# Cross-attention: one four-bank PSUM tile becomes four tiles, and some work of the other engines moves

## The chip, the cores and the metric

The kernel runs on one core of a Trainium2 chip. A core has five engines that run side by side, each through its own queue in order: TensorE (PE in the profile; its weight loads are PEld), VectorE (DVE), ScalarE (ACT), GpSimd (POOL) and SyncE (SP, which here only issues DMAs). TensorE writes its results to PSUM; the kernel's four banks of sums lie there. The metric is the device time of one execution in microseconds (us), lower is better.

## The reference

For each of 64 sequences (256 rows of queries `x`, 512 wide; 256 rows of context `c`, 384 wide), in float32:

```python
text_p  = einsum('bld,dh->blh', x, W_text) + b_text      # 512 -> 512
audio_p = einsum('bsd,dh->bsh', c, W_audio) + b_audio    # 384 -> 512
Q = layer_norm(text_p, g1, beta1)
K = layer_norm(audio_p, g2, beta2)
V = audio_p
scores = einsum('blh,bsh->bls', Q, K) / sqrt(512)
alpha  = softmax(scores, axis=-1)
hyper  = einsum('blh,hk->blk', einsum('bls,bsh->blh', alpha, V), W_out) + b_out
return layer_norm(hyper + x, g_out, beta_out)
```

## The kernel before

The whole program is unrolled, with its order written by hand: the order of the calls in the source is the order in each engine's queue, and the framework adds the semaphore waits that the data need. One sequence is one round of the main loop (line 1027), and a round works on several sequences at once. In round `b` it computes keys (`k2`) and queries (`q2`) of sequence `b + 2`, the scores and the exponentials of `b` (`at`), the context (`alpha` times `c`) of `b - 1` (`last`), the output product of `b - 2` (`old.o`), and the closing layer norm and store of `b - 3` (`settled`).

The value product and `W_out` are folded at the start (`fold_multiply`): the context rows are multiplied by `W_audio W_out`. So there are three large products for a sequence.

- Keys and output rows go through the class `Thirds` (line 482): a product of 2 by 3 by 3 blocks with 15 block products in place of 18. Its sums are 172 wide, and there are eight of them: L0, L1, M0, M1, N0, N1, T, U. TensorE adds products to them in five steps, `one` (N), `two` (M), `three` (T), `four` (M, L, T), `five` (N, M, U). Between these, VectorE works on the sums in PSUM: `after_one` (copy N1, write T), `after_three` (copy T, write L), `after_four` (write U). `after_five`, `leave` and `leave_plus` take the results out. `seed` (line 508) writes the bias into M before `two`. Keys and output share the same sums, one after the other in the round.
- Queries go through the class `Fork` (line 569): a product of 2 by 2 by 2 blocks with 7 block products, with sums in two further banks (`fork`). `first`, `six`, `five`, `rest` are its steps on TensorE; `after_first` copies two of the sums on ScalarE. `square`, `scales` and `normalise` make the layer norm; the rows are scaled where they leave PSUM.

The eight sums of `Thirds` lie in one PSUM tile of four banks (line 65), at these places:

```python
third = p_all.tile([P, 4, H], F32, tag="third", name="ps_t")
L0, M0 = third[:, 0, :W3], third[:, 0, W3 : 2 * W3]
T, U = third[:, 1, :W3], third[:, 1, W3 : 2 * W3]
L1, M1 = third[:, 2, :W3], third[:, 2, W3 : 2 * W3]
N0, N1 = third[:, 3, :W3], third[:, 3, W3 : 2 * W3]
```

Normalised queries and keys are stored to DRAM (`qd`, `kd`) and fetched again in squares (`qq`, `kq`) that VectorE's transposing instruction turns (`turn`, lines 74 and 453) into `qT` and `kT`; ScalarE then applies gamma and beta to them (`affine`, line 469). The exponentials take the same way (`ed`, `eq`, `turn_e`, `eT`). Inputs come as rows (`x`, `c`) and as squares (`xq`, `cq`), the squares four rounds ahead. All of these DMAs are issued by SP, in this order in a round: `eq`, `x`, `c`, `cq`, `xq`, `qd`, `kd`, `qq`, `kq`, `ed`, `out`.

GpSimd makes the sums of blocks that the fast products need: `third_sides` (line 306) for keys (`csum`) and for the output (`zsum`), `sum_x` (line 290) for queries (`xsum`); it also makes the reciprocal square roots (`rstd_of`, line 362) and part of the rows.

Of the kernel before, what the change touches and what calls it, by code (L numbers as in the profile page):

```python
# [9 lines left out]
F32 = mybir.dt.float32  # L10
AF = mybir.ActivationFunctionType
ALU = mybir.AluOpType
# [3 lines left out]
P = 128  # L16
# [6 lines left out]
def kernel(  # L23
# [18 lines left out]
    nc = tc.nc  # L42
    ctx.enter_context(tc.manual_schedule())
    B, L, D = x.shape
    S, DA = c.shape[1:]
    H = w_text.shape[1]
    LT, ST = L // P, S // P
    DC, AC, HC = D // P, DA // P, H // P
    scale = 1.0 / math.sqrt(H)
    W3 = -(-H // 12) * 4  # L50
# [11 lines left out]
    p_all = ctx.enter_context(tc.tile_pool(name="p_all", bufs=1, space=PSUM))  # L62
    p_at = ctx.enter_context(tc.tile_pool(name="p_at", bufs=2, space=PSUM))

    third = p_all.tile([P, 4, H], F32, tag="third", name="ps_t")
    fork = p_all.tile([P, 2, H], F32, tag="fork", name="ps_f")

    def squares(dst, src):
# [163 lines left out]
    wao_sb = wao_pad[:, :, :D]  # L232
# [4 lines left out]
    def fold_multiply(a, lo=0, hi=HC):  # L237

        for k in range(lo, hi):
            nc.tensor.matmul(  # L240
                third[:, a, :],
                lhsT=waT[k][:, bass.ts(a, P)],
                rhs=wo_sb[:, k, :],
                start=(k == 0),
                stop=(k == HC - 1),
            )

    def fold_evict(a):
        nc.scalar.copy(wao_sb[:, a, :], third[:, a, :])

    def fold_bias(part):

        ps = third[:, 3, :]
        nc.tensor.matmul(ps, lhsT=ones, rhs=part, start=True, stop=True)
        nc.vector.tensor_copy(bao_sb, ps)

# [222 lines left out]
    def dve(o, i0, i1, op):  # L479
        nc.vector.tensor_tensor(o, i0, i1, op)  # L480

    class Thirds(Projection):

        L0, M0 = third[:, 0, :W3], third[:, 0, W3 : 2 * W3]
        T, U = third[:, 1, :W3], third[:, 1, W3 : 2 * W3]
        L1, M1 = third[:, 2, :W3], third[:, 2, W3 : 2 * W3]
        N0, N1 = third[:, 3, :W3], third[:, 3, W3 : 2 * W3]
        L, M, N = third[:, 0:3:2, :W3], third[:, 0:3:2, W3 : 2 * W3], third[:, 3, : 2 * W3].rearrange("p (n h) -> p n h", n=2)

        def __init__(self, name, b, sides, weights, bias, delta):  # L490
            self.name, self.b, self.nt, self.centred = name, b, 2, True
# [37 lines left out]
        def after_one(self):  # L529
            n1 = self.room("n1")  # L530
            nc.vector.tensor_copy(n1, self.N1)  # L531
            dve(self.T, self.N0, n1, ALU.subtract)
# [9 lines left out]
            dve(m, self.M1, self.delta, ALU.subtract)  # L542
            dve(self.U, self.M0, m, ALU.subtract)

        def after_five(self):
            u, n = self.room("u"), self.room("n", 2)
            nc.scalar.copy(u, self.U)
            nc.scalar.copy(n, self.N)  # L548
            dve(self.rows[:, 0, W3 : 2 * W3], self.T, u, ALU.add)
            dve(self.ends(1), self.M, n, ALU.add)  # L550
            d = self.room("d")
            nc.gpsimd.tensor_tensor(d, n[:, 0], n[:, 1], ALU.subtract)  # L552
            nc.gpsimd.tensor_tensor(self.rows[:, 1, W3 : 2 * W3], u, d, ALU.add)

        def ends(self, t):
            return self.padded[:, t].rearrange("p (j h) -> p j h", j=3)[:, 0:3:2]
# [12 lines left out]
    class Fork(Projection):  # L569
# [20 lines left out]
            self.product(1, self.R)  # L590
            self.product(7, self.q2)

        def after_first(self):
            nc.scalar.copy(self.q1, self.R)
            self.s7 = once.tile([P, H2], F32, tag="s7", name="s7")
            nc.scalar.copy(self.s7, self.q2)  # L596

# [34 lines left out]
    class Attention:  # L632
# [114 lines left out]
            self.y = self.o.rows  # L747

        def statistics(self, lo=0, n=LT):

            self.nm = small.tile([P, LT], F32, tag="nm", name="nm")
            self.ssq = small.tile([P, LT], F32, tag="ssq", name="ssq")
            self.summed = range(lo, lo + n)
            for t in self.summed:
                junk = work.tile([P, D], F32, tag="junk", name="junk")
                nc.scalar.activation(  # L756
                    junk, self.y[:, t, :], AF.Identity, scale=-1.0 / D, accum_out=self.nm[:, t : t + 1]
                )
            for t in self.summed:
                junk = work.tile([P, D], F32, tag="junk", name="junk")  # L760
                nc.scalar.activation(  # L761
                    junk,
                    self.y[:, t, :],
                    AF.Square,
                    bias=self.nm[:, t : t + 1],
                    accum_out=self.ssq[:, t : t + 1],
                )
            self.r = dict(zip(self.summed, rstd_of(self.ssq[:, lo : lo + n], n, total=True)))
# [137 lines left out]

    assert B > 4 and AC == 3
    q, k, xT, cT, xs, cs, att = {}, {}, {}, {}, {}, {}, {}
    bank = [third[:, n, :] for n in range(4)] + [fork[:, n, :] for n in range(2)]

    c_turn = RowTurn(c_0, AC, "cT")
    x_turn = RowTurn(x_0, DC, "xT")
# [77 lines left out]
    k[0].affine(g2_sb, be2_sb)  # L990
    q[1] = Fork(1, xs.pop(1), wt_blocks)
    q[1].first()
    q[1].after_first()
    part = bias_parts()
    fold_multiply(2, 0, 2)
    q[1].six()
# [22 lines left out]
    wao_room = const.tile([P, HC * H], F32, tag="wo", name="wao_thirds")  # L1019
    wao_t = wao_room[:, : 11 * W3].rearrange("p (n h) -> p n h", n=11)  # L1020

    def start_queries(b):
        q[b] = Fork(b, xs.pop(b), wt_blocks)
        q[b].first()
        q[b].after_first()

    for b in range(B - 2):
        at = att[b] = att.get(b) or Attention(b)
        settled, old, last = att.pop(b - 3, None), att.get(b - 2), att.get(b - 1)
        three = b + 3 < B  # L1030
        if last:
            last.fetch_e()
        if b > 1:
            load_x_rows(b - 1)
            load_c_rows(b - 1)
        if b + 4 < B:
            load_c(b + 4)
            load_x(b + 4)
        if b == 1:
            go_sb = row(g_out, "go")  # L1040
            beo_sb = row(beta_out, "beo")
        if b == 0:
            at.score(0, 8)
            Fork.seed()
        k2 = k[b + 2] = Thirds("k", b + 2, cs.pop(b + 2), wa_blocks, ba_pad, ba_delta)
        if b == 0:
            k2.seed()
        k2.one()
        k2.after_one()
        k2.two()  # L1050
        if b == 0:
            start_queries(2)
        q2 = q[b + 2]
        if old:
            old.context_two(0)
        k2.three()
        if old:
            old.context_two(1)
            old.copy_two()
        if three:  # L1060
            cT[b + 3] = turn_c(b + 3)
        if b:
            at.affine_keys()
        k2.after_three()
        if old:
            old.start_products()
        if three:
            cs[b + 3] = third_sides(cT.pop(b + 3), "csum")
        q2.six()
        q2.after_six()  # L1070
        k2.four()
        k2.after_four()
        q2.five()
        q2.after_five()
        if last:
            last.turn_e()
        if b:
            at.affine_queries()
        k2.five()
        if settled:  # L1080
            settled.statistics()
        k2.after_five()
        q2.rest()
        k2.leave()
        if old:
            old.o.seed()
        q2.square()
        q2.scales()
        q[b + 1].turn()
        if three:  # L1090
            xT[b + 3] = turn_x(b + 3)
        if b:
            at.score(0, 2)
        if old:
            old.o.one()
            old.o.after_one()
            old.o.two()
        if b:
            at.score(2, 3)
        if old:  # L1100
            old.o.three()
        k[b + 1].turn([0])
        k2.square()
        k2.scales()
        if old:
            old.o.after_three()
        k[b + 1].turn([1])
        if not three:
            att[b + 1] = Attention(b + 1)
            att[b + 1].affine_queries()  # L1110
        if b:
            at.score(3, 6)
        q2.normalise()
        q2.store()
        if old:
            old.o.four()
        if settled:
            settled.shift(0)
            settled.shift(1)
        if old:  # L1120
            old.o.after_four()
        if b:
            at.score(6, 8)
        if old:
            old.o.five()
        if three:
            Fork.seed()
        k2.normalise()
        k2.store()
        q2.fetch()  # L1130
        k2.fetch()
        if three:
            xs[b + 3] = sum_x(xT.pop(b + 3))
        if b < 2:
            wao_blocks = third_weights(wao_pad, wao_t, [b])
        at.maxima()
        at.exponentials()
        if not three:
            att[b + 1].affine_keys()
        if settled:  # L1140
            settled.settle(0)
        if old:
            old.o.after_five()
        if three:
            start_queries(b + 3)
        at.reciprocals()
        if old:
            old.o.leave_plus(x_rows[b - 2])
        if last:
            last.context_one()  # L1150
        at.divide_e()
        if three:
            k2.seed()
        at.store_e()
        if last:
            last.copy_one()
        if settled:
            settled.settle(1)
            settled.store()

    settled, old, last = att[B - 5], att[B - 4], att[B - 3]
    at = att[B - 2]
# [46 lines left out]
    q[B - 1].affine(g1_sb, be1_sb)  # L1209
    end = Attention(B - 1)  # L1210
    old.o.five()
    old.o.after_five()
    old.o.leave_plus(x_rows[B - 4])
    last.o.seed()
    at.context()
# [17 lines left out]
    end.reciprocals()  # L1233
    old.statistics()
    last.o.five()
    last.o.after_five()
    last.o.leave_plus(x_rows[B - 3])
    end.transpose_e(bank[5])
    end.copy_e()
# [65 lines left out]
```

## Time and profile before

| what | value |
| --- | --- |
| median of 2 runs | 1824.55 us (1824.04 to 1825.06) |
| the profiled execution | 1824.55 us, its span 1822.8 us |
| mean granted TensorE clock | 0.931 |
| ScalarE copies of `s7` (L596), first to last of 63 | 48.9 to 1719.5 us |
| the chain of work that ended last, by engine | PE 54%, ACT 26%, DVE 8%, DMA 6% |
| DMA, share of the 16 engines' time | 71.3%, mean 177 GB/s |

A line of the profile names the engine, the source line, the tile written and the tiles read, and how often. `ps_t` is the tile `third`, `ps_f` is `fork`, `ps_sc` the scores, `ps_z` the context. A number in brackets behind a line of the timeline is the time that the engine sat idle before it, and what released it. The clock is that which the chip granted to TensorE, 1.00 being full speed. A call of the matmul shows as two rows.

### The profile page before, as it was taken

The numbers are of one execution on the slowest core, as the hardware profiler recorded it, in microseconds if no ns is written. First come the engines' busy times: TensorE is split into PE (matmuls) and PEld (weight loads), VectorE is DVE, ScalarE is ACT, GpSimd is POOL, SyncE is SP. The second block draws the span as 40 slices with busy tenths as digits, with TensorE's granted clock in tenths as the row PEclk, the third lists the DMA queues.
The fourth block names the chain that finished last, engine by engine and source line by source line (L and its number), as shares of the span: only waits on it lengthen the run. The fifth ranks groups of instructions, "written<-read, shape, count | busy, mean of one in ns | idle before, by whom it ended". The sixth has DMA issues, their size and how long they took to land.

```text
span 1822.8 us, 25850 instructions
## 1 busy us (share of the span) xinstructions
PE 1572.8 (86%) x7419; PEld 1314.6 (72%) x7419; DVE 1077.5 (59%) x2248; ACT 1143.7 (63%) x2929; POOL 1139.2 (62%) x1946
## 2 busy tenths in 40 slices
PE   7798988988988988988988988988988988988965
PEld 3577777777777777777777777777777777777753
DVE  4355665665665666665665665665665665665545
ACT  3466666666666667666666666666666666666651
POOL 4766566566566566566566566566566566566534
PEclk9899999999999999999999999999999999999988
DMA  7586767777877877877777777767777877777641
GB/s 186 122 191 167 202 173 174 202 174 174 203 173 175 203 171 179 200 170 179 198 173 180 195 175 181 198 172 181 197 172 181 199 171 181 197 173 179 168 142 47
DMA packets 450453, 322.51 MB, mean 177 GB/s; under 512 B 154885, under 2 KB 382981, under 8 KB 450310
## 3 DMA queue, kind: packets, MB, share of 16 engines
q1 hardware_dynamic: 450214, 320.72, 71.3%
q8 instruction: 59, 0.97, 0.2%
q14 instruction: 84, 0.69, 0.1%
q10 hardware_dynamic: 96, 0.13, 0.0%
HBM read 203.83 MB, written 116.92 MB: 176 GB/s over the span
## 4 chain that ended last, share of the span: by engine, by line
PE 54%; ACT 26%; DVE 8%; DMA 6%; issue 3%; POOL 1%; SPq 1%; DVEq 0%; ACTq 0%; POOLq 0%
PE ps_t L499 28%; PE ps_f L585 11%; PE ps_sc L650 11%; ACT junk L620 4%; ACT qT L471 3%; ACT kT L471 3%; PE ps_z L716 3%; ACT e L681 3%; ACT ps_t L509 3%; DVE ps_t L480 2%; DMA c<-in_ctx_dram 2%; DVE n L531 2%; ACT junk L756 2%; DVE kr L480 2%; ACT junk L761 2%
## 5 line engine op out<-in xcount | busy, mean ns | idle before, releaser
L650 PE MATMUL ps_sc<-kT,qT 128*128 128x256 f32 x1024 | 309.4, 432 | 4.2 <-ACT zT L731 4.2
L552 POOL TENSOR_TENSOR d<-n 128x172 f32<-128x172 f32 x124 | 68.1, 549 | 298.1 <-ACT n L548 293.4
L499 PE MATMUL ps_t<-wao,zsum 128*128 128x172 f32 x496 | 141.7, 424 | 128.1 <-DVE ps_t L480 71.7
L650 PEld LDWEIGHTS ps_sc<-kT,qT 128*128 128x128 f32 x1024 | 228.1, 231 | 26.5 <-ACT zT L731 5.0
L311 POOL TENSOR_TENSOR zsum<-zT 128x256 f32<-128x256 f32 x124 | 73.3, 591 | 242.8 <-ACT zT L734 231.5
L499 PEld LDWEIGHTS ps_t<-wao,zsum 128*128 128x128 f32 x496 | 101.0, 251 | 166.4 <-DVE ps_t L480 87.9
L667 ACT ACTIVATE e<-ps_sc,nmx 128x256 f32<-128x256 f32 x128 | 59.4, 469 | 238.2 <-DVE nmx L660 238.2
L585 PE MATMUL ps_f<-wtsum,xsum 128*128 128x256 f32 x756 | 197.0, 384 | 1.0 <-ACT s L596 0.6
L716 PE MATMUL ps_z<-eT,c 128*128 128x256 f32 x768 | 197.1, 381 | 0.8 <-ACT eT L705 0.8
L499 PE MATMUL ps_t<-wao_thirds,zsum 128*128 128x172 f32 x744 | 184.9, 347 | 2.5 <-DVE ps_t L480 2.5
L499 PE MATMUL ps_t<-wa,csum 128*128 128x172 f32 x496 | 107.5, 340 | 79.6 <-DVE ps_t L480 54.4
L499 PE MATMUL ps_t<-wa_thirds,csum 128*128 128x172 f32 x744 | 173.1, 328 | 0.0
L499 PEld LDWEIGHTS ps_t<-wao_thirds,zsum 128*128 128x128 f32 x744 | 142.1, 213 | 39.1 <-DVE ps_t L480 24.5
L499 PEld LDWEIGHTS ps_t<-wa,csum 128*128 128x128 f32 x496 | 74.6, 193 | 121.0 <-DVE ps_t L480 70.8
L536 DVE COPY t<-ps_t 128x172 f32<-128x172 f32 x124 | 41.8, 337 | 202.4 <-PE ps_t L499 202.4
L585 PEld LDWEIGHTS ps_f<-wtsum,xsum 128*128 128x128 f32 x756 | 143.1, 193 | 19.2 <-ACT s L596 0.9
L499 PEld LDWEIGHTS ps_t<-wa_thirds,csum 128*128 128x128 f32 x744 | 121.6, 191 | 42.7 <-DVE ps_t L480 39.5
L716 PEld LDWEIGHTS ps_z<-eT,c 128*128 128x128 f32 x768 | 141.5, 192 | 14.4 <-ACT eT L705 1.0
L734 ACT COPY zT<-ps_z 128x256 f32<-128x256 f32 x64 | 23.8, 372 | 199.5 <-PE ps_z L716 199.5
L370 POOL TENSOR_TENSOR rstd<-ve,nhalf 128x2 f32<-128x2 f32 (+1 forms) x192 | 136.1, 709 | 16.0
L585 PE MATMUL ps_f<-wt,xT 128*128 128x256 f32 x504 | 132.5, 386 | 10.2 <-ACT ps_f L581 10.2
L480 DVE TENSOR_TENSOR kr<-ps_t,u 128x172 f32<-128x172 f32 x62 | 20.9, 337 | 190.9 <-ACT n L548 114.4
(196 smaller groups left out, 4056.7 us busy)
## 6 DMA issues: line engine op xcount, KB each, us to landing
kd<-kr SPq DMA_DIRECT2D x64, 512.0 KB, 3.2
kq<-kd SPq DMA_DIRECT2D x256, 128.0 KB, 3.9
qd<-qr SPq DMA_DIRECT2D x64, 512.0 KB, 2.8
qq<-qd SPq DMA_DIRECT2D x256, 128.0 KB, 3.5
xq<-in_x_dram SPq DMA_DIRECT2D x252, 128.0 KB, 5.3
x<-in_x_dram SPq DMA_DIRECT2D x63, 512.0 KB, 4.2
out_dram<-yr SPq DMA_DIRECT2D x62, 512.0 KB, 3.1
cq<-in_ctx_dram SPq DMA_DIRECT2D x252, 96.0 KB, 5.4
```

Of the source, the lines that this page charges most:

```text
L311: less = lambda o, i0, i1: nc.gpsimd.tensor_tensor(o, i0, i1, ALU.subtract)
L370: nc.gpsimd.tensor_tensor(r, ve, nhalf[:, :n], ALU.pow)
L471: nc.scalar.activation(self.T[:, k, :], self.T[:, k, :], AF.Identity, bias=bet[:, k : k + 1], scale=gam[:, k : k + 1],)
L480: nc.vector.tensor_tensor(o, i0, i1, op)
L499: nc.tensor.matmul(place, lhsT=self.sides[n], rhs=self.weights[n], start=(n == 14), stop=True, skip_group_check=True,)
L509: nc.scalar.copy(self.M, self.bias.rearrange("p (j h) -> p j h", j=3)[:, 0:3:2])
L552: nc.gpsimd.tensor_tensor(d, n[:, 0], n[:, 1], ALU.subtract)
L585: nc.tensor.matmul(place, lhsT=side, rhs=w, start=False, stop=True, skip_group_check=True)
L620: nc.scalar.activation(junk, fork[:, t, :], AF.Square, scale=1.0 / math.sqrt(H), accum_out=self.var[:, t : t + 1],)
L650: nc.tensor.matmul(self.sc[:, t, :], lhsT=self.qT[:, k, bass.ts(t, P)], rhs=self.kT[:, k, :], start=(k == 0), stop=(k == HC - 1),)
L667: nc.scalar.activation(self.e[:, t, :], self.sc[:, t, :], AF.Exp, bias=self.nmx[:, t : t + 1], accum_out=self.den[:, t : t + 1],)
L716: nc.tensor.matmul(ps, lhsT=c_rows[self.b][:, s, bass.ts(j, P)], rhs=self.eT[:, s, :], start=(s == 0), stop=(s == ST - 1),)
```

## The change

The four banks become four tiles of their own, named m, l, u and n. Each holds a pair side by side: M0 and M1, L0 and L1, T and U, N0 and N1. The copies of `u` and `n` in `after_five` take the engine as an argument: ScalarE for keys, VectorE for the output in the main loop. The GpSimd part of it becomes `middle`. `after_first` of the queries is cut into `after_one` and `after_seven`, and `statistics` of the closing layer norm into `sums` and `deviations`. In the loop, `sums` go to the head of the round and `deviations` behind the scaling of the keys; the queries of sequence `b + 1` are scaled by gamma and beta in round `b`, between the squares and `normalise` of `q2`; GpSimd's `csum` goes behind `middle` of the keys; the squares of the keys go ahead of those of the queries; both `settle` go to the end of the round. The number of matmuls and of DMAs stays.

```diff
-    third = p_all.tile([P, 4, H], F32, tag="third", name="ps_t")
+    third = [p_all.tile([P, H], F32, tag=f"t{n}", name=f"ps_{n}") for n in "mlun"]
...
-        L0, M0 = third[:, 0, :W3], third[:, 0, W3 : 2 * W3]
-        T, U = third[:, 1, :W3], third[:, 1, W3 : 2 * W3]
-        L1, M1 = third[:, 2, :W3], third[:, 2, W3 : 2 * W3]
-        N0, N1 = third[:, 3, :W3], third[:, 3, W3 : 2 * W3]
-        L, M, N = third[:, 0:3:2, :W3], third[:, 0:3:2, W3 : 2 * W3], third[:, 3, : 2 * W3].rearrange("p (n h) -> p n h", n=2)
+        M, L, TU, N = [t[:, : 2 * W3].rearrange("p (n h) -> p n h", n=2) for t in third]
+        M0, M1, L0, L1 = M[:, 0], M[:, 1], L[:, 0], L[:, 1]
+        T, U, N0, N1 = TU[:, 0], TU[:, 1], N[:, 0], N[:, 1]
...
-        def after_five(self):
-            u, n = self.room("u"), self.room("n", 2)
-            nc.scalar.copy(u, self.U)
-            nc.scalar.copy(n, self.N)
-            dve(self.rows[:, 0, W3 : 2 * W3], self.T, u, ALU.add)
-            dve(self.ends(1), self.M, n, ALU.add)
+        def after_five(self, copy):
+            self.u, self.n = self.room("u"), self.room("n", 2)
+            copy(self.u, self.U)
+            copy(self.n, self.N)
+            dve(self.rows[:, 0, W3 : 2 * W3], self.T, self.u, ALU.add)
+            dve(self.ends(1), self.M, self.n, ALU.add)
+
+        def middle(self):
             d = self.room("d")
-            nc.gpsimd.tensor_tensor(d, n[:, 0], n[:, 1], ALU.subtract)
-            nc.gpsimd.tensor_tensor(self.rows[:, 1, W3 : 2 * W3], u, d, ALU.add)
+            nc.gpsimd.tensor_tensor(d, self.n[:, 0], self.n[:, 1], ALU.subtract)
+            nc.gpsimd.tensor_tensor(self.rows[:, 1, W3 : 2 * W3], self.u, d, ALU.add)
...
     for b in range(B - 2):
...
+        if settled:
+            settled.sums()
         k2.one()
         k2.after_one()
         k2.two()
...
         if old:
             old.start_products()
-        if three:
-            cs[b + 3] = third_sides(cT.pop(b + 3), "csum")
         q2.six()
         q2.after_six()
+        if settled:
+            settled.deviations()
         k2.four()
...
             last.turn_e()
-        if b:
-            at.affine_queries()
         k2.five()
-        if settled:
-            settled.statistics()
-        k2.after_five()
-        q2.rest()
+        k2.after_five(nc.scalar.copy)
         k2.leave()
+        k2.middle()
+        if three:
+            cs[b + 3] = third_sides(cT.pop(b + 3), "csum")
         if old:
             old.o.seed()
+        q2.rest()
+        k2.square()
         q2.square()
         q2.scales()
+        k2.scales()
         q[b + 1].turn()
...
         k[b + 1].turn([0])
-        k2.square()
-        k2.scales()
         if old:
             old.o.after_three()
...
             at.score(3, 6)
+        q[b + 1].affine(g1_sb, be1_sb)
         q2.normalise()
         q2.store()
...
-        if settled:
-            settled.settle(0)
         if old:
-            old.o.after_five()
+            old.o.after_five(nc.vector.tensor_copy)
+            old.o.middle()
         if three:
-            start_queries(b + 3)
+            q3 = q[b + 3] = Fork(b + 3, xs.pop(b + 3), wt_blocks)
+            q3.first()
+            q3.after_one()
         at.reciprocals()
...
         at.divide_e()
         if three:
+            q3.after_seven()
             k2.seed()
         at.store_e()
         if last:
             last.copy_one()
         if settled:
+            settled.settle(0)
             settled.settle(1)
             settled.store()
```

## The prediction

> **What bounds the kernel now.** I read the page first: busy time by engine and the clock row.
>
> ```profile
> span 1822.8 us, 25850 instructions
> PE 1572.8 (86%) x7419; PEld 1314.6 (72%) x7419; DVE 1077.5 (59%) x2248; ACT 1143.7 (63%) x2929; POOL 1139.2 (62%) x1946
> PEclk9899999999999999999999999999999999999988
> ```
>
> No engine but PE is above 63%, and PE itself never gets its whole clock: its mean is 0.931 in every slice. So the bound is PE with something that takes time from it in every round of the main loop. The copies of `s7` (L596) stand 27.31 us apart from 135.08 to 1719.5 us: 58 equal rounds. The timeline of PE over one of them, 899.9 to 927.2 us, with its idle time in brackets, is:
>
> ```profile
> 901.90 0.85 PE L499 MATMUL ps_t<-wa,csum 128*128 128x172 f32 x4 [0.33 <-ACT ps_t L509]
> 903.63 0.85 PE L499 MATMUL ps_t<-wa,csum 128*128 128x172 f32 x4 [0.88 <-DVE ps_t L480]
> 913.08 1.03 PE L650 MATMUL ps_sc<-kT,qT 128*128 128x256 f32 x4
> 915.06 0.82 PE L499 MATMUL ps_t<-wao,zsum 128*128 128x172 f32 x4 [0.95 <-POOL ve L366]
> 916.93 1.52 PE L499 MATMUL ps_t<-wao,zsum 128*128 128x172 f32 x4 [1.05 <-DVE ps_t L480]
> ```
>
> These four gaps, 0.33 + 0.88 + 0.95 + 1.05 = 3.21 us, are all the idle time of the round, and each stands before `one` or `two` of a `Thirds`. `one` writes N (fourth bank); what releases it is ACT's `seed` (L509), which writes M (first and third bank). `two` writes M; what releases it is DVE's subtraction that writes T (second bank). The third gap names POOL, but that `ve` ended at 914.58; the `seed` of the output ended at 914.96, 0.1 us before the matmul. So PE waits for an access to another bank of the same tile. The list of PE's waits has it for the whole run:
>
> ```profile
> PE ps_t L499 <- DVE ps_t L480: 128.6, 127, 8.0
> PE ps_t L499 <- POOL ve L366: 54.1, 57, 1.0
> PE ps_t L499 <- ACT ps_t L509: 25.2, 62, 3.2
> ```
>
> Then stretches of 1 us (PE's busy time, then PEld, DVE, ACT, POOL, clock, DMA share, GB/s):
>
> ```profile
> 915.90:916.90 1.00, 0.00 (x0) 0.00 (x0) 0.97 (x4) 1.00 (x5) 0.77 (x2) 0.99 0.03 5
> 916.90:917.90 1.00, 0.97 (x3) 0.97 (x4) 0.59 (x1) 0.73 (x3) 0.92 (x3) 0.50 0.00 0
> 918.90:919.90 1.00, 1.00 (x4) 0.91 (x4) 0.00 (x0) 0.97 (x3) 0.92 (x2) 0.50 0.06 20
> 919.90:920.90 1.00, 1.00 (x5) 0.83 (x5) 0.92 (x3) 0.89 (x2) 1.00 (x3) 0.81 1.01 385
> ```
>
> Right after the last two gaps the clock is 0.50 for about 3.41 us (0.81 in the last row is 0.38 us of 0.50), which costs half of that, 1.71 us. The 3.41 us before hold the last two gaps, 2.00 us, so 41% work; a stretch that holds the first two, 1.21 us, has 65%, and there the clock stayed 1.00. 27.31 is eight times 3.41: the rounds are locked to these stretches, one slow in eight.
>
> What is left is PE's floor: 27.31 - 3.21 - 1.71 = 22.4 us a round.
>
> **The change, part by part.**
>
> *Four tiles.* `k2.one` no longer waits for the seed of M: the 0.33 goes. `two` no longer waits for T: 0.88 and 1.05 go. `o.one` needs only the copy of N (ended 913.15 while PE still scored) and follows the scores at 914.0: 0.95 goes. The chain N1 copy, T (0.35 + 0.35 and two handovers, 0.88) now lies under `two` (0.58) and `context_two(0)` or `score(2,3)` (0.43). `leave` reads L beside DVE's reading of M, and its 0.88 us of waiting on ACT goes. Sum on PE: 3.21, plus 1.71 if the clock then holds, which the 65% lets me expect if no stretch sinks to some 41%.
>
> [...]
>
> *Queries scaled a round ahead.* Four ACT instructions, 1.97 us (907.92 to 909.89), leave the place before `after_five`, where they made ACT late: `five` had ended by 910.5, ACT copied `u` at 912.52. They go between `q2.square` and `q2.normalise`. Nothing is added in number, but `q2.normalise`, the store of `qd` behind it and, on SP, everything queued behind that now wait for them.
>
> *Statistics in two halves.* The sums (1.22) go to the head of the round, where ACT sat idle 3.31 us before `zT` (L734): free. The squares (1.41) stay before `u`; `rstd` goes ahead on POOL; both `settle` go to the end of the round. Only output waits for that.
>
> *POOL.* `csum` (910.19 to 914.31, 4.1 us) goes behind `middle`. Then come the scales of queries and keys. PE without gaps ends `five` 7.4 us into the round (`one` and `two` 1.2, then `context_two` to `five` as it ran, 904.32 to 910.49, 6.2); `n` is copied at 8.1, then `middle` 1.25, `csum` 4.15 and the scales 0.98 give `q2.r` at 14.5. ACT could be there at 13.7 (sums 0.8, seed, squares and scaled queries 4.8 behind `n`) and waits 0.8 if `eT` is in time. What PE needs of it, the fork's seed (`normalise` 1.29 and 0.52 later, 16.3), it needs at `first`, 22.4 - 3.4 = 19 us into the round: covered by 2.7 us; with that gone, it adds to the round directly.
>
> *Output copies of `u`, `n` on DVE.* ACT loses 0.29 + 0.45. A DVE copy of 128x172 took 0.34 (L536), DVE over 128x344 0.51 (L480): 0.85 more on DVE at the round's end. Queued behind them: two sums 0.76, reciprocal, `leave_plus` 0.56. Under these PE runs `first` and `context_one`, 3.44 us, before anything needs M: covered by about 1 us. Without that cover `two` is late by the excess.
>
> **What is late next.** With PE faster, a loop that goes through SP closes. SP's queue of the round:
>
> ```profile
> 918.93 0.38 SPq L442 DMA_DIRECT2D qd<-qr  x1
> 920.87 0.38 SPq L442 DMA_DIRECT2D kd<-kr  x1
> 921.78 3.56 SPq L72 DMA_DIRECT2D qq<-qd  x4
> 926.15 1.78 SPq L72 DMA_DIRECT2D kq<-kd  x4
> 928.84 0.38 SPq L685 DMA_DIRECT2D ed<-e  x1
> 931.25 1.80 SPq L72 DMA_DIRECT2D eq<-ed  x4
> 936.39 5.32 SPq L72 DMA_DIRECT2D xq<-in_x_dram  x4
> ```
>
> `ed` stands behind `kq`, `eq` behind `ed`'s landing; `turn_e` waits for `eq` on DVE, and behind it queue `after_five`'s sums; the output's `seed` waits for those on M; behind the seed on ACT queue the squares, the scaled queries and `normalise`, which releases the next `qd`. Step by step: `qd` to the end of `kq` 918.93 to 927.93, 9.00; to `ed` 0.05; `ed` to the first `eq` 2.41; to the last `eq` landed 3.75 (last issue 932.6, 2.4 to land); `turn_e` 0.75; the two sums 0.76 (913.24 to 914.00); seed 0.41; key squares 1.23; query squares 1.15; scaled queries 1.97; `normalise` to `qd` 1.29. Sum 22.8 us, just over PE's floor. Before, the same loop had slack: `eq` landed at 935.0, `turn_e` ran at 936.7.
>
> Two terms may grow, as the DMA queues lose their rest. The loads of `xq` drained 12.4 us after the first `eq` (DMA share 0.31 at 943 to 944, then 0.00 for 3 us); the loop puts `qd` 11.3 after it: 0 to 1.1 more, I take 0.5, the middle. `ed` now goes right behind `kq`, not 0.9 us later: 0 to 0.9, I take 0.4. So 22.8 + 0.9 = 23.7 us a round. On PE it shows as a wait of `o.three`, whose T comes behind `turn_e` and the transposes on DVE.
>
> The profiled execution had 1822.8 us of span and 1.75 outside it, 1824.55, which is the median of the two runs. 58 x (27.31 - 23.7) = 209; 1824.55 - 209 = 1615 us. Prologue, first rounds and epilogue I leave as they are: each has a few such gaps and nothing that grows.
>
> **Rivals.**
>
> *PE's floor decides.* If SP's issues go quicker when they are asked for earlier (`qq` took 3.56 us for four, `kq` 1.78 for as many), the loop falls below 22.4 us. Time 1824.55 - 58 x 4.9 = 1540. For it: that difference of 1.78 us alone is more than the loop stands above the floor. Against: `qq` would be asked for into fuller queues, not emptier ones.
>
> *The loop grows to 24.5 to 27 us.* `o.three`'s wait of 1 to 2 us could again bring a stretch to half clock (1.7 us), or `csum` hold the scales. 1824.55 - 58 x 2.8 = 1662, up to 1807.
>
> *Slower: the DMA round trips.* The page's last part has `qq` at 3.5 us to landing, `cq` 5.4, `c` 5.9, where `ed` and `eq` have 2.3 and 2.1: these land fast because the queues are nearly empty then. If in the tighter round each of the loop's four trips (`qd`, `kd`, `ed`, `eq`) takes `cq`'s 5.4, the loop gains 2.6 + 2.2 + 3.1 + 3.3 = 11.2 at most; half of that gives 22.8 + 5.6 = 28.4 us a round, 1824.55 + 58 x 1.1 = 1888. It makes the kernel slower by over 2% from 27.9 us on, 5.1 us above my sum. Against it: 177 GB/s now would be 204 at 23.7 us a round, and some rows move 385.
>
> *It does not do what it says.* The waits could stay, if what orders them is not the tile; or the clock could hold the round at eight stretches: 27.31, 1825.
>
> **How the numbers follow.** My loop (23.2 to 24.2 us) 0.50; PE's floor 0.17; the longer loop 0.20, of which 0.02 is within 2%; DMA trips 0.08; no effect 0.05. The range takes in the floor and the longer loop up to 25.4 us (1824.55 - 58 x 1.9 = 1714): 1538 to 1714, leaving out some 0.2. Faster by over 2% (2% is about what a measurement of this kernel tells from no change): 0.50 + 0.17 + 0.18 = 0.85; within 2%: 0.07; slower 0.08.
>
> **What would show it.** In the changed profile PE's waits for `seed` (L509) and for T before `two` are gone; the clock is 1.00 through the round; `s7`'s copies stand 23 to 24 us apart; DVE waits for `eq` before `turn_e`, SP's `ed` follows `kq` at once, and PE's one larger gap is before `o.three`. I am wrong if rounds stand at 22.4 with no wait for `eq`, if a 0.50 stretch stays in every round, or if `qd`, `ed` or `eq` land more than 2 us later than now.

## The result and the profile after

| | before | after |
| --- | --- | --- |
| median of 2 runs | 1824.55 us (1824.04 to 1825.06) | 1521.25 us (1519.05 to 1523.45) |
| ratio, 95% interval | | 0.8338 [0.8285, 0.839] |
| span of the profiled execution | 1822.8 us | 1517.2 us |
| mean round (copies of `s7`, the last 58) | 27.32 us | 22.52 us |
| idle time of PE in a mean round | 3.23 us | 0.72 us |

The kernel takes a sixth less time, and 94 us less than forecast: 1521 lies below the lower end of the range, 1538. The mechanism was the one forecast; the sizes of its terms, and the ends of the program, were not. The top of the page of after, in the places shown of before, with the share of the main DMA queue and the chain of work that ended last:

```profile
span 1517.2 us, 26098 instructions
...
PE 1427.3 (94%) x7419; PEld 1228.5 (81%) x7419; DVE 1125.0 (74%) x2368; ACT 1106.3 (73%) x2809; POOL 1211.2 (80%) x1946
...
PEclk9999999999999999999999999999999999999988
...
q1 hardware_dynamic: 450214, 320.72, 85.5%
...
PE 37%; DMA 17%; DVE 17%; POOL 12%; ACT 6%; issue 5%; SPq 4%; DVEq 0%; ACTq 0%; POOLq 0%
```

The clock row looks the same as before, since a 9 stands for 90% or more; the mean granted clock went from 0.931 to 0.988, and the stretch from 1000 to 1100 us has 1.00 where it had 0.94. PE is busy 94% of the span, but it holds only 37% of the chain that ended last, where it had 54%. DMA, DVE and POOL together hold 46% of it: the chain runs around through the other engines.

The timeline of PE at the two steps `one` and `two`, first of keys and then of the output (start, duration, engine, line, operation, tiles, count; in brackets the idle time before it and its releaser):

```profile
910.75 0.75 PE L497 MATMUL ps_n<-wa,csum 128*128 128x172 f32 x4
911.33 0.75 PE L497 MATMUL ps_m<-wa,csum 128*128 128x172 f32 x4
...
921.57 0.75 PE L497 MATMUL ps_n<-wao,zsum 128*128 128x172 f32 x4
922.15 0.75 PE L497 MATMUL ps_m<-wao,zsum 128*128 128x172 f32 x4
922.73 0.59 PE L652 MATMUL ps_sc<-kT,qT 128*128 128x256 f32 x2
923.61 0.53 PE L497 MATMUL ps_u<-wao_thirds,zsum 128*128 128x172 f32 x2 [0.28 <-DVE ps_u L480]
```

None of the four gaps is left: `two` starts 0.58 us behind `one`, where it stood 1.73 us behind (901.90 to 903.63). The one gap of this round is the one that the prediction named, before `o.three`. SP's queue of the same round:

```profile
904.18 0.38 SPq L442 DMA_DIRECT2D qd<-qr  x1
906.11 0.38 SPq L442 DMA_DIRECT2D kd<-kr  x1
907.05 1.95 SPq L72 DMA_DIRECT2D qq<-qd  x4
909.32 1.78 SPq L72 DMA_DIRECT2D kq<-kd  x4
911.21 0.40 SPq L687 DMA_DIRECT2D ed<-e  x1
911.71 0.41 SPq L896 DMA_DIRECT2D out_dram<-yr  x1
915.12 1.98 SPq L72 DMA_DIRECT2D eq<-ed  x4
```

`ed` is issued 0.11 us after `kq`, and the first `eq` 3.91 us after `ed`. And the row of `turn_e` on DVE, before and then after (lists of groups: count, busy time and mean ns, idle time before it):

```profile
L75 DVE STREAM_TRANSPOSE eT<-eq 128x512 f32<-128x512 f32 x62 | 43.5, 702 | 7.2 <-DMA eq<-ed 7.2
...
L75 DVE STREAM_TRANSPOSE eT<-eq 128x512 f32<-128x512 f32 x62 | 44.1, 711 | 143.4 <-DMA eq<-ed 143.4
```

DVE waits 143.4 us for `eq`, 2.3 us in the mean of 62 times; before, it was 7.2 us in all. So the loop over SP, slack before, is closed. The longest of PE's own waits are short against that:

```profile
PE ps_u L497 <- DVE ps_u L480: 26.6, 38, 1.5
PE ps_f L585 <- ACT ps_f L581: 15.8, 4, 6.4
PE ps_u L497 <- POOL csum L311: 7.2, 7, 1.1
```

Where the 305.6 us of the span came from: 58 rounds of 4.80 us less, 278; the first copy of `s7` stands 8.3 us earlier (48.9 to 40.6), the first four rounds took 5.1 us less (86.2 to 81.1), and what follows the last copy 13.9 us less (103.2 to 89.3).

### The profile page after: what moved, and what is told of

The parts are those of the page before. It is cut to its first block, busy times and chain, and to the rows that moved or that the text cites. A ratio compares the mean times of both kernels' runs of the same rounds, so it can differ in the third digit from the quotient of the medians.

```text
span 1517.2 us, 26098 instructions
## 1 busy us (share of the span) xinstructions
PE 1427.3 (94%) x7419; PEld 1228.5 (81%) x7419; DVE 1125.0 (74%) x2368; ACT 1106.3 (73%) x2809; POOL 1211.2 (80%) x1946
## 4 chain that ended last, share of the span: by engine, by line
PE 37%; DMA 17%; DVE 17%; POOL 12%; ACT 6%; issue 5%; SPq 4%; DVEq 0%; ACTq 0%; POOLq 0%
DMA ed<-e 10%; PE ps_f L585 9%; PE ps_m L497 7%; PE ps_sc L652 6%; DMA eq<-ed 5%; SPq L72 4%; PE ps_u L497 4%; PE ps_z L718 4%; PE ps_n L497 3%; DVE qT L75 3%; DVE xT L75 3%; DVE yr L877 3%; DMA kd<-kr 2%; POOL csum L311 2%; PE ps_l L497 2%
## 5 line engine op out<-in xcount | busy, mean ns | idle before, releaser
L652 PE MATMUL ps_sc<-kT,qT 128*128 128x256 f32 x1024 | 261.0, 379 | 2.6 <-ACT zT L733 2.6
L75 DVE STREAM_TRANSPOSE eT<-eq 128x512 f32<-128x512 f32 x62 | 44.1, 711 | 143.4 <-DMA eq<-ed 143.4
L471 ACT ACTIVATE kT<-kT,columns 128x256 f32<-128x256 f32 x256 | 132.9, 592 | 0.0
L471 ACT ACTIVATE qT<-qT,columns 128x256 f32<-128x256 f32 x256 | 132.4, 593 | 0.4 <-DVE qT L75 0.4
L585 PEld LDWEIGHTS ps_f<-wt,xT 128*128 128x128 f32 x504 | 93.6, 192 | 27.5 <-ACT ps_f L581 17.6
L877 DVE SCALAR_TENSOR_TENSOR yr<-yr,nm,go 128x512 f32<-128x512 f32 x122 | 111.7, 954 | 0.7 <-ACT junk L770 0.7
L310 POOL TENSOR_TENSOR csum<-csum,cT 128x256 f32<-128x256 f32 x186 | 99.2, 548 | 9.7
L886 DVE SCALAR_TENSOR_TENSOR yr<-yr,rstd,beo 128x512 f32<-128x512 f32 x124 | 106.0, 894 | 1.2 <-POOL rstd L370 1.2
L310 POOL TENSOR_TENSOR zsum<-zsum,zT 128x256 f32<-128x256 f32 x186 | 99.1, 547 | 9.7
L567 POOL TENSOR_TENSOR yr<-yr,x 128x512 f32<-128x512 f32 x62 | 105.7, 1705 | 0.0
L480 DVE TENSOR_TENSOR ps_l<-ps_m,t 128x172 f32<-128x172 f32 x248 | 85.6, 345 | 17.4 <-ACT zT L736 0.5
```

Of the source, the lines that this page charges most:

```text
L75: nc.vector.transpose(dst.rearrange("p k (b j) -> p b k j", j=SQ), src.rearrange("p b (k i) -> p b k i", k=chunks),)
L310: plus = lambda o, i0, i1: nc.gpsimd.tensor_tensor(o, i0, i1, ALU.add)
L471: nc.scalar.activation(self.T[:, k, :], self.T[:, k, :], AF.Identity, bias=bet[:, k : k + 1], scale=gam[:, k : k + 1],)
L567: add(self.rows[:, 1], self.rows[:, 1], x[:, 1], ALU.add)
L585: nc.tensor.matmul(place, lhsT=side, rhs=w, start=False, stop=True, skip_group_check=True)
L652: nc.tensor.matmul(self.sc[:, t, :], lhsT=self.qT[:, k, bass.ts(t, P)], rhs=self.kT[:, k, :], start=(k == 0), stop=(k == HC - 1),)
```

## The experiments

**Theory.** The waits inside the four-bank tile were most of the cost; with them gone, SP's loop (`qd`, `qq`, `kq`, `ed`, `eq`, `turn_e`, sums, seed, squares, scaled queries, `normalise`, `qd`) sets the round, not PE. **Rivals.** The moves of the other engines' work made the gain; or one of the four banks apart would do; or PE is at its floor, and the loop only rides along.

Each kernel was timed beside the kernel before on the same chip, in three sittings; the medians of the kernel before there were 1820.2 to 1822.2 us. The kernel after was not timed again, so a difference of some us from its 1521.25 is not told from none. The rounds and the clock are those of one profiled execution each.

| kernel | median us | ratio [95%] | clock | mean round us |
| --- | --- | --- | --- | --- |
| `e1_tiles_only` | 1551.84 | 0.8517 [0.8499, 0.8535] | 0.987 | 23.07 |
| `e2_moves_only` | 1704.42 | 0.9358 [0.9339, 0.9378] | 0.987 | 25.29 |
| `e5_u_apart` | 1777.18 | 0.9767 [0.9752, 0.9781] | 0.955 | 26.61 |
| `e6_n_apart` | 1717.24 | 0.9440 [0.9424, 0.9456] | 0.958 | 25.65 |
| `e3_ed_ahead` | 1481.27 | 0.8130 [0.8113, 0.8147] | 0.988 | 21.94 |
| `e4_turn_later` | 1511.87 | 0.8295 [0.8278, 0.8312] | 0.989 | 22.39 |
| `e8_both` | 1464.47 | 0.8049 [0.8036, 0.8062] | 0.989 | 21.61 |
| `e9_ed_behind_out` | 1589.33 | 0.8714 [0.8685, 0.8742] | 0.980 | 23.64 |
| `e7_affine_back` | 1534.49 | 0.8436 [0.8419, 0.8452] | 0.984 | 22.86 |
| `e11_csum_back` | 1592.18 | 0.8743 [0.8719, 0.8768] | 0.983 | 23.71 |
| `e10_copies_act` | 1518.56 | 0.8336 [0.8319, 0.8353] | 0.988 | 22.50 |

### The tiles alone, and the moves alone

`e1_tiles_only` is the kernel before with four tiles and nothing moved:

```diff
-    third = p_all.tile([P, 4, H], F32, tag="third", name="ps_t")
+    third = [p_all.tile([P, H], F32, tag=f"t{n}", name=f"ps_{n}") for n in "mlun"]
...
+        M, L, TU, N = [t[:, : 2 * W3].rearrange("p (n h) -> p n h", n=2) for t in third]
```

> The kernel before with the four tiles and the pairs of sums in one bank, nothing else moved. If the waits between banks of one tile were the loss (theory): the four gaps of 3.21 us a round and the half-clock stretch of 1.71 us go, and what is late next is ScalarE, which still has queries, keys and statistics (6.6 us) ahead of the copy of u, so that T of the output comes about 1.3 us late: rounds of 23 to 24 us, time 1560 to 1610 us, clock above 0.97. If the moved work carries most of the gain (rival): rounds above 25.5 us, time above 1700 us.

1551.84 us, 8 us below the range. One gap of 1.06 us in the mean is left in a round, before `o.three`, and PE's waits for the seed and for T before `two` are gone from the rounds:

```profile
PE ps_u L497 <- DVE ps_u L480: 61.8, 59, 1.4
```

`e2_moves_only` is the kernel after with the sums in the one tile of before:

```diff
-    third = [p_all.tile([P, H], F32, tag=f"t{n}", name=f"ps_{n}") for n in "mlun"]
+    third = p_all.tile([P, 4, H], F32, tag="third", name="ps_t")
```

> The changed kernel with its sums in one tile of four banks again, at the old places. Theory: the gaps before one and two stay (about 3 us a round), and with them a half-clock stretch in most rounds; rounds of 25 to 27.3 us, time 1700 to 1830 us, clock 0.93 to 0.95. Rival (the moves carry the gain): below 1650 us.

1704.42 us: in the range, but the clock is whole, which was not expected. The timeline of PE shows the gaps, before `two` and `five` of the output and before `one` and `two` of the keys. All are still released by work on another bank (`five` begins with N and waits for U), but each large one has at least 5 us of work on one side of it:

```profile
907.08 0.85 PE L499 MATMUL ps_t<-wao,zsum 128*128 128x172 f32 x4 [0.88 <-DVE ps_t L480]
...
913.33 0.85 PE L499 MATMUL ps_t<-wao_thirds,zsum 128*128 128x172 f32 x4 [0.89 <-DVE ps_t L480]
...
918.72 0.85 PE L499 MATMUL ps_t<-wa,csum 128*128 128x172 f32 x4 [0.21 <-ACT ps_t L509]
920.45 0.85 PE L499 MATMUL ps_t<-wa,csum 128*128 128x172 f32 x4 [0.88 <-DVE ps_t L480]
```

So a round of 27.3 us becomes 25.3 by the moves alone, 23.1 by the tiles alone and 22.5 by both. The first rival, that the moves made the gain, falls: most of it is the tiles. The two parts overlap, in part because each frees the clock by itself (0.987 in both). A round less its idle time on PE is 24.09 us before (27.32 - 3.23) and 22.44 in `e2_moves_only` (25.29 - 2.85), with four gaps in each: 1.65 us is what the half clock cost, where the prediction had 1.71. The new tiles also pair the sums differently (M0 beside M1, where L0 stood beside M0). The pairing by itself was not tried, but the two kernels that follow have it too, with three banks still in one tile, and they keep 3.37 and 3.12 us of gaps a round: the pairing does not remove the waits.

### One bank apart

`e5_u_apart` is the kernel before with T and U in a tile of their own and M, L, N together; `e6_n_apart` has N apart and M, L, T, U together:

```diff
-    third = p_all.tile([P, 4, H], F32, tag="third", name="ps_t")
+    third_mln = p_all.tile([P, 3, H], F32, tag="tmln", name="ps_mln")
+    third_u = p_all.tile([P, 1, H], F32, tag="tu", name="ps_u")
+    third = [third_mln[:, 0, :], third_mln[:, 1, :], third_u[:, 0, :], third_mln[:, 2, :]]
```

> The kernel before in its own order, with T and U in a tile of their own and M, L, N together in another. The waits of two for T go (0.88 and 1.05 us), those of one for the seed stay (0.33 and 0.95). Theory: a half-clock stretch needs some 2 us of idle time in 3.41; one gap of 0.95 leaves 72% work, so the clock is whole (above 0.98): rounds of 23.3 to 24.0 us, 1565 to 1610 us. Rival (the half-clock stretch hangs on something else than these gaps): clock about 0.93, rounds above 25 us, above 1690 us.

> The kernel before in its own order, with N0 and N1 in a tile of their own and M, L, T, U together in another. The waits of one for the seed go (0.33 and 0.95 us), those of two for T stay (0.88 and 1.05). Theory: the two gaps stand 14 us apart, one alone leaves 69% work in a stretch of 3.41 us, so the clock is whole (above 0.98): 27.31 - 1.28 - 1.71 = 24.3 us a round, up to 25 with T of the output late, 1620 to 1670 us. Rival: clock about 0.93, above 1730 us.

The first missed wholly: 1777 us, with all four gaps in place and a fifth of 0.5 us before `o.five`. PE's waits in it:

```profile
PE ps_mln L499 <- DVE ps_u L482: 139.8, 151, 9.4
PE ps_mln L499 <- ACT ps_mln L509: 79.1, 121, 3.2
```

In it, `two` writes M and still waits for the subtraction that writes T, although T now lies in another tile. That subtraction also reads N0, and N lies in the tile of M. So here a read of one bank held a write to another bank of its tile, as a write did: the first row, 139.8 us. The second was half right: the gap at `one` went, but the one at `two` of the output grew to 2.23 us, and the clock is not whole (0.958). Stretches of 1 us around that gap (PE, PEld, DVE, ACT, POOL, clock, DMA share, GB/s), in one round and in the next:

```profile
908.00:909.00 1.00, 0.12 (x1) 0.00 (x0) 1.00 (x2) 1.00 (x4) 0.86 (x2) 1.00 1.23 191
909.00:910.00 1.00, 0.00 (x0) 0.00 (x0) 0.90 (x3) 1.00 (x4) 0.92 (x3) 1.00 0.89 150
910.00:911.00 1.00, 0.65 (x4) 0.65 (x5) 0.91 (x2) 0.83 (x4) 0.83 (x3) 0.98 0.14 31
911.00:912.00 1.00, 1.00 (x5) 0.82 (x4) 0.00 (x0) 0.69 (x2) 0.92 (x3) 0.50 0.00 0
...
936.00:937.00 1.00, 0.33 (x2) 0.34 (x3) 0.90 (x3) 0.90 (x3) 0.83 (x3) 1.00 0.00 0
937.00:938.00 1.00, 1.00 (x8) 0.95 (x7) 0.22 (x1) 0.62 (x3) 0.92 (x3) 1.00 0.03 8
938.00:939.00 1.00, 1.00 (x7) 0.90 (x6) 0.68 (x2) 0.97 (x3) 1.00 (x2) 1.00 0.00 0
```

After the first gap of 2.2 us (908.12 to 910.35) the clock is 0.50; after the second, 26 us later and as long (2.22), it stays 1.00. The last section shows where the two lie in the stretches of the clock. In most of the program the rounds alternate between 24.9 and 26.3 us. The rival that one bank apart would do falls: in the first all the waits stay, and in the second those between the three banks that still share a tile grow. The work itself needs none of them: in `e1_tiles_only` the same instructions run on four banks without these waits, and one gap of 1.06 us a round is left.

### SP's loop

`e3_ed_ahead` is the kernel after with the fetch of the keys' squares behind the store of `ed`, so that `ed` doesn't wait for `kd` to land and `kq` to be issued:

```diff
         q2.fetch()
-        k2.fetch()
...
         at.store_e()
+        k2.fetch()
```

> The changed kernel with the fetch of the keys (kq, four DMAs) issued behind the store of the exponentials (ed) instead of ahead of it. Theory (the loop qd, qq, kq, ed, eq, turn_e, sums, seed, squares, queries, normalise sets the 22.5 us): ed goes out 1.9 us less late and lands sooner (2.3 us rather than 3.9), the loop falls to about 19.5 to 20.6 us, and TensorE's own work (the shortest rounds seen, 21.6 us) decides: 58 x 0.9 = 52 us less, 1460 to 1480 us; VectorE no longer waits for eq. Rival (TensorE's floor already decides): 1513 to 1529 us.

1481.27 us, 40 us less than the kernel after: 1 us above the range of the theory, and far from the rival. SP's queue shows the other order:

```profile
908.68 0.38 SPq L687 DMA_DIRECT2D ed<-e  x1
909.15 1.92 SPq L72 DMA_DIRECT2D kq<-kd  x4
911.17 0.49 SPq L896 DMA_DIRECT2D out_dram<-yr  x1
911.76 2.61 SPq L72 DMA_DIRECT2D eq<-ed  x4
```

From `ed` to the first `eq` it is 3.08 us here (3.30 in the mean), with `kq` and `out` issued in between. More than half of the rounds take 21.6 us. The reverse, `ed` issued behind the output's store (`e9_ed_behind_out`), lengthens the loop:

```diff
-        at.store_e()
...
             settled.store()
+        at.store_e()
```

> The changed kernel with the store of the exponentials (ed) issued behind the store of the output (out), the other way from the run that put it ahead of kq. Theory (the loop over SP sets the round): ed goes out 0.5 us later, and lands up to 1.3 us later behind the 512 KB of out: rounds of 23.0 to 24.3 us, 1550 to 1625 us. Rival (TensorE's floor decides): 1513 to 1530 us.

1589.33 us, with 1.12 us more a round. In the mean, `ed` is issued 0.69 instead of 0.10 us behind `kq`, and the first `eq` follows it after 4.54 instead of 3.89 us: 0.59 + 0.65 = 1.24, about the whole of it. Both directions answer as a loop must.

`e4_turn_later` takes `turn_e` out of its place ahead of the keys' last sums on DVE, so that these no longer queue behind the wait for `eq`:

```diff
-        if last:
-            last.turn_e()
         k2.five()
...
         k[b + 1].turn([1])
+        if last:
+            last.turn_e()
```

> The changed kernel with turn_e behind the second half of the keys' transposes on VectorE, so that the sums behind five no longer queue behind eq. Theory: the loop is opened at another link, ed still goes out behind kq and lands in 3.9 us, but nobody on the way to TensorE waits for it: rounds of 21.4 to 21.7 us, 1455 to 1480 us. Rival (TensorE's floor already decides): 1513 to 1529 us.

It missed: 1511.87 us, 9 less than after (the intervals of the two ratios overlap) instead of 41 to 66. The wait for `eq` is gone, as DVE's timeline shows, but the new place is in front of another chain:

```profile
919.21 0.70 DVE L464 STREAM_TRANSPOSE kT<-kq 128x512 f32<-128x512 f32 x1
919.84 0.67 DVE L75 STREAM_TRANSPOSE eT<-eq 128x512 f32<-128x512 f32 x1
920.43 2.34 DVE L877 SCALAR_TENSOR_TENSOR yr<-yr,nm,go 128x512 f32<-128x512 f32 x2
922.70 0.32 DVE L480 TENSOR_TENSOR m<-ps_m,bao_delta 128x172 f32<-128x172 f32 x1
```

The two subtractions that write U of the output (the second at 923.13) stand behind `turn_e` and the 2.34 us of the shifts. They read M, and inside `o.five` PE waits for them before it adds to M:

```profile
923.53 0.85 PE L497 MATMUL ps_m<-wao_thirds,zT 128*128 128x172 f32 x4 [1.00 <-DVE ps_u L480]
```

That wait stands 58 times, 29.8 us in all. So `e8_both` puts `turn_e` behind these subtractions, after the maxima, and keeps `ed` ahead:

```diff
-        if last:
-            last.turn_e()
...
-        k2.fetch()
...
         at.maxima()
+        if last:
+            last.turn_e()
...
         at.store_e()
+        k2.fetch()
```

> The changed kernel with kq fetched behind ed, and with turn_e behind maxima, where VectorE stood idle 0.7 us (not ahead of the shifts, where it made U of the output 1 us late). Theory: both links are out, TensorE's own work decides in every round: 21.4 to 21.7 us, 1445 to 1470 us. Rival (another wait takes over, as in the run with turn_e moved alone): 1475 us or more.

1464.47 us, the fastest of all, 57 us below the kernel after. The mean round is 21.61 us, with 0.09 us of idle time on PE. Its page:

```profile
span 1460.6 us, 26343 instructions
...
PE 1408.7 (96%) x7419; PEld 1226.3 (84%) x7419; DVE 1115.2 (76%) x2368; ACT 1105.7 (76%) x2809; POOL 1196.8 (82%) x1946
...
PE 78%; DVE 10%; POOL 5%; issue 3%; DMA 1%; ACT 1%; SPq 0%; DVEq 0%; POOLq 0%; ACTq 0%
```

Here PE holds 78% of the chain and DMA 1%; in the kernel after it was 37% and 17%. So 21.6 us is PE's floor with this order, and the kernel after stood 0.9 us above it: the rival that PE was already at its floor falls.

### The other moves, one at a time

Three kernels take back one move each of the kernel after. `e7_affine_back` scales the queries in their own round again, behind `turn_e`:

```diff
+        if b:
+            at.affine_queries()
         k2.five()
...
-        q[b + 1].affine(g1_sb, be1_sb)
+        if not three:
+            q[b + 1].affine(g1_sb, be1_sb)
```

> The changed kernel with the queries scaled in their own round again, ahead of the copies of u and n. Theory: the copies come at 919.1 instead of 918.3, still about when turn_e ends (919.9), the 1.97 us leave the loop, but normalise then waits for the scales that stand behind csum on GpSimd: rounds of 22.3 to 23.1 us, 1510 to 1555 us, so this part of the change is worth nothing or little. Rival (it is worth its 1.97 us): above 1600 us.

`e11_csum_back` puts `csum` back behind the start of the output:

```diff
             old.start_products()
+        if three:
+            cs[b + 3] = third_sides(cT.pop(b + 3), "csum")
...
         k2.middle()
-        if three:
-            cs[b + 3] = third_sides(cT.pop(b + 3), "csum")
```

> The changed kernel with csum on GpSimd at its old place, ahead of the keys' middle and behind zsum. Theory: the keys' middle ends about 4.1 us later (924.2 rather than 920.2), the squares of the keys wait for it and stand ahead of those of the queries, so normalise comes some 2 to 2.6 us later and the loop grows by that: rounds of 24.5 to 25.1 us, 1635 to 1675 us. Rival (the place of csum does not matter, TensorE decides): below 1540 us.

`e10_copies_act` lets ScalarE copy `u` and `n` of the output again:

```diff
-            old.o.after_five(nc.vector.tensor_copy)
+            old.o.after_five(nc.scalar.copy)
```

> The changed kernel with the output's copies of u and n on ScalarE again, as before. Theory: neither engine's work there lies on the loop; 0.75 us leave VectorE and 0.63 come to ScalarE, where it waited 1.4 us for first: 1505 to 1530 us. Rival (the move to VectorE was part of the gain): above 1540 us.

Queries scaled a round ahead are worth some 13 us by the medians (1534.49 against 1521.25); between the two profiled executions it is 0.34 us a round. `csum` behind `middle` is worth 71 us, the largest of the three, though only about half of what I expected: 1.2 us a round. Without it, the other moves make the kernel slower than the tiles alone (rounds of 23.71 against 23.07 us): the moves lean on one another, and those not listed here were not taken apart. With it in its old place, `middle` on POOL comes late, and behind that the second square of the keys on ACT:

```profile
919.35 0.63 ACT L404 ACTIVATE junk<-kr 128x512 f32<-128x512 f32 x1 [1.35 <-POOL kr L553]
```

That square lies in the loop, between the seed and `normalise`. From `turn_e` to `qd` the loop then takes 8.72 us in the mean, where it is 7.54: the 1.18 us are the whole difference of a round (23.71 - 22.52). The copies on DVE are worth nothing that shows: 1518.56 us (1515.77 to 1520.27).

## Why the prediction was right and where it failed

**Right.** The waits for another bank of the same tile are gone, and `e1_tiles_only` shows that the tiles alone remove them. The half-speed stretch is gone from the round, for about the price predicted (1.65 measured, 1.71 said). The loop that I named is what set the next bound: `ed` follows `kq` at once, DVE waits for `eq`, and PE's gap is before `o.three`. `e3_ed_ahead` and `e9_ed_behind_out` show it from both sides. The rounds themselves (22.52 us, not 23 to 24) lie nearer to the 22.4 that the prediction had for PE's floor than to its loop; it is the wait for `eq` and these two kernels that tell loop from floor, not the time.

**The step that failed** is the first term of the loop, "`qd` to the end of `kq` 918.93 to 927.93, 9.00". It was read off one round, and that round was an odd one: its four `qq` took 3.56 us and `kq` stood 0.81 us behind them, while over 54 rounds of before the means are 2.07 and 0.43. In the same odd round `ed` stood 0.91 us behind `kq`, where the mean is 2.7, so the term from `ed` to the first `eq` was taken to grow by 0.4 us where it grew by 1.6. The loop's terms as predicted, beside the means over 55 rounds of after, in us:

| term | predicted | measured |
| --- | --- | --- |
| `qd` to the end of `kq` | 9.00 | 3.00 + 2.03 + 0.36 + 1.90 = 7.29 |
| `qd` late, behind the loads of `xq` | 0.50 | 0 (0.13 at most, in the 3.00) |
| `kq` to `ed` | 0.05 | 0.10 |
| `ed` to the first `eq` | 2.41 + 0.40 = 2.81 | 3.89 |
| first `eq` to `turn_e` | 3.75 | 3.70 |
| `turn_e` to the next `qd` | 7.56 | 7.54 |
| sum | 23.67 | 22.52 |

Two terms were 1.71 and 0.50 too large, one was 1.08 too small; the last two, over half of it the work of DVE and ACT summed from the rows of before, held to 0.05 us. The rival that had the loop quicker argued from this very difference between `qq` and `kq`, and I set it aside by an argument about fuller queues where the rows of a second round would have settled it. Net 1.15 us a round, over 58 rounds 67 us of the error.

That the loop was named rightly is in part luck. With the means of before in the first term (2.86 + 2.07 + 0.43 + 1.82 = 7.19 us) and the other terms as they stood, the sum is 21.9 us, below the 22.4 that the prediction had for PE's floor, and it would have had to name the floor as what decides. The loop stands above the floor because `ed` took 1.08 us longer than taken, and because the floor is lower than taken.

**PE's floor** was put at 22.4 us; it is 21.6 or less. I took off a gap's idle time alone. But without the gap the next start comes 0.58 us after that of `one`, before the 0.85 us that its matmuls stand for are over: 1.73 - 0.58 = 1.15 us saved where I counted 0.88. Four such ends of 0.27 are 1.08 us, and 22.4 - 1.08 = 21.3 stands close to the 21.52 of `e8_both` (21.61 less 0.09 idle). With the right floor, the loop stood 0.9 us above it. The lower end of the range, 1538, came from the floor too (the first rival's 1540); with 21.5 us in it, it would have been some 1490.

**The ends of the program** were left as they were, "each has a few such gaps and nothing that grows". They gave 27 us: 8.3 + 5.1 + 13.9. In the tail, the timeline of PE before has two waits of the same kind, each some ten times as long as one in a round (at the first, `two` waits for T; at the second, PE is to write two banks while DVE still reads a third):

```profile
1763.53 1.52 PE L499 MATMUL ps_t<-wao,zsum 128*128 128x172 f32 x4 [8.04 <-DVE ps_t L480]
...
1809.52 5.34 PE L831 MATMUL ps_t<-wao,zT 128*128 128x256 f32 x12 [9.49 <-DVE y L787]
```

Neither is left in the kernel after, whose tail has other waits instead (6.8 us for a load of `c`, 1.5 us before a step of the output). `e1_tiles_only` has a tail of 90.7 us, `e2_moves_only` of 99.7, the kernel before of 103.2, and the wait for `y` is still 9.5 us in `e2_moves_only`: here too it is mostly the tiles. They were to be read in the same trace. 67 + 27 us is, to 2 us, the distance from 1615 to the profiled execution, 1519 (the median is 1521). Either of the two alone would have left the time inside the range.

**Half right.** I tied the clock to the four gaps being closed by the tiles. `e2_moves_only` keeps 2.85 us of gaps a round at a clock of 0.987, where the kernel after has 0.988; its gaps are spread, at most 0.21 + 0.88 us of them within 3.41 in the round shown. The prediction did set idle time against stretches of 3.41 us, but it then asked only whether gaps go, not whether they move apart. Nor is 0.931 the clock of every slice, as its first reading has it: it is the mean of the whole execution, and in the rounds the clock is 1.00 but for the one stretch of 0.50. The DMA rival, four trips at 5.4 us, did not come: only `ed` lands later, by 1.6 us (2.27 us to the first `eq` before, 3.89 after). Nor were the queues nearly empty for `ed` and `eq` before, as it has them: in the microsecond ahead of each the DMA share was 0.59 (`ed`) and 1.02 (first `eq`) in the mean of 55 rounds.

**Open.** Why the first `eq` follows `ed` after 3.9 us when `ed` stands right behind `kq`, and after 3.3 when it stands ahead, is not settled. What is issued just before `ed` is not all of it: `e8_both` has the order of `e3_ed_ahead`, and there the mean is 3.6. Of the 13 us at the start and in the first rounds, which waits gave them was not taken apart. Rounds of 22 to 24 us among the 21.6 of `e3_ed_ahead` were not followed up; `e8_both` has a single one above 22 (22.1).

## What to carry to other kernels

Give every PSUM bank that is written and read on its own a tile of its own: the waits that the framework adds between engines went by the tile here, and a read of one bank held a write to another (`e5_u_apart`, 139.8 us of waits). When a stall that recurs in every round is removed, sum the loop that runs through the in-order queue issuing the DMAs, with each term a mean over many rounds and not one round's row; then put whatever waits for a DMA behind the work that doesn't. Count a gap as the distance between two starts, and look for the same wait in the prologue and the tail: in the tail of the kernel before it was 8.0 and 9.5 us, against 0.3 to 1.1 us in a round.

## What the runs showed of the hardware

The half clock came with less idle time than a whole stretch of 3.41 us, and it depended on where the idle time fell. In the kernel before, two gaps of 0.95 and 1.05 us with 0.82 us between them cost one stretch of 3.41 us at 0.50 in 57 of the 58 rounds. In `e6_n_apart` a single gap of 2.2 us cost one in the first of the two rounds shown and none in the second; its mean clock, 0.958, lies between the 0.931 of before and the 0.988 of after. In `e2_moves_only` four gaps of 0.2 to 0.9 us, 2.85 us a round but at most 1.1 within 3.41 in the round shown, left the mean clock at 0.987.

In the profiles of before and after the stretches lay on a fixed grid: their clock records hold 134 and 10 starts of a stretch at one clock, and within each profile all of them lie within 0.002 us of one grid of 3.4133 us. Divided along this grid, the last 58 rounds of the two give 407 and 382 stretches at full clock. Of the 732 with 1.65 us or less of idle time on PE none was followed by a slow stretch, and the 57 with 1.92 us or more, all of before, all were; none lay between. So in these two the idle time counted by its sum within one stretch. `e6_n_apart` agrees: its slow stretch ran from 910.96 to 914.38 us, so on such a grid the first of the two gaps shown lies whole in the stretch from 907.55 us, and the second is split, 0.41 and 1.81 us, by the line at 934.86.

The rounds of before fit the grid too: their mean of 27.32 us is eight such stretches (8 x 3.413 = 27.31), so that in each round the slow one met the same gaps. In `e6_n_apart` two rounds, 24.9 + 26.3 = 51.2 us, are fifteen of them. That the grid holds the rounds at these lengths was not tried by itself.

`ed`, a store of 256 KB, landed later where it was issued closer behind other DMAs of its queue: it took 2.27 us to the first `eq` when issued 2.7 us behind `kq` (before, mean of 54 rounds), 3.89 at 0.10 us behind it (after), and 4.54 behind the output's store as well (`e9_ed_behind_out`). The rounds grew shorter between the first and the second too, so the distance in the queue is not shown to be the only cause.
